# A two-block image network on one core: v's copies, weight preparation and the pacing of layer norms re-ordered

## The chip, the core and the metric

The kernel runs on one core of a Trainium2 chip. The time is that of the device, in microseconds, from the first to the last instruction of one launch; three runs of the kernel before give a median of 3362.36 us (3358.76 to 3363.83).

A core has five engines that run side by side, each with its own list of instructions in a fixed order: TensorE (PE) multiplies matrices, VectorE (DVE) and ScalarE (ACT) work element by element, GpSimd (POOL) and SyncE (SP) here mostly issue DMAs. They meet through semaphores: an instruction stands at the head of its engine's list until what it needs is there, and all that is behind it waits too.

## What is computed

Eight images of 384 channels and 32 x 32 places (1024 tokens) go through two blocks, all in float32:

```python
# block 0: attention and MLP on tokens
xn = layernorm(x, g1, beta1)
q, k, v = xn @ w_qkv.T + b_qkv                 # 8 heads of 48
x1 = softmax(q @ k.T * SCALE) @ v @ w_proj.T + b_proj + x
y = x1 + gelu(layernorm(x1, g2, beta2) @ w_fc1.T + b_fc1) @ w_fc2.T + b_fc2
# block 1: depthwise 7x7 convolution, norm, GELU, global response norm
z = layernorm(dwconv7x7(y) + dw_b, ln_w, ln_b)
z = gelu(z @ w1 + b1)
nx = l2norm_over_places(z); nx = nx / (mean(nx) + eps)
out = y + (gamma * z * nx + beta + z) @ w2 + b2
```

## The kernel before

**Layout.** Channels lie on the 128 partitions (three tiles of 128), tokens along the free dimension. An image's half is 512 tokens, a quarter of the first image 256. Attention works through two query halves (`qh`) times four pairs of heads (`m`) times eight key tiles (`t`). The exponential of scores runs on ScalarE, the convolution as 147 multiply-add taps for each image on VectorE.

**The order of work.** Images overlap: while TensorE does attention and the MLP of image b, VectorE convolves image b-1. The order of each engine's list is fixed when the program is built, by hand. Side work (a layer norm, a convolution, the preparation of weights) is written as a generator that yields how many us of matmul time to leave before its next step. `Flow.pe(us)` is called after each matmul, adds the normal time of it to a clock and lets all steps that are due write their instructions at this point of the program. So a longer wait moves a step further back in the lists, in whole matmul steps (0.857 us for one of 512 columns, 1.714 in `linear`); it doesn't make any engine idle by itself. `flow.finish` writes all remaining steps at once. `after(first, chain, us)` starts a chain when another one has ended. A chain spawned as `paced` counts its waits from the time when its last step was due.

**Layer norm.** `layernorm` has the same eight steps everywhere: two additions over the channel tiles (L406, L409), a sum over partitions by a matmul with ones (L374, or L388 when `fold` first halves the rows with a DMA, L382), subtraction of the mean (L416), squares on ScalarE (L423), their additions (L427, L430), the variance by a matmul, logarithm and exponential on ScalarE (L440, L441), and the scaling (L444). `slow` stretches some of its waits; `abreast` runs both halves side by side and stretches all of them by `factor`.

**The start.** `first_values` normalises image 0 in quarters, two steps apart, and computes v for each quarter (L521, two tiles of 128 tokens), copied out by ScalarE (L529).

**Weights prepared in image 0.** `folds` folds the norms' beta into biases: VectorE weighs the weights (L238, L240), TensorE sums them in columns (L244, 128x1 matmuls). `prepare(weights, False)` loads blocks of weights into the buffer `acc`, builds 15 sums of blocks ("forms", L1182, L1185) for a multiplication of matrices with fewer products, stores them in DRAM, and builds sums of w1. `prepare(weights, True)`, called `aside`, folds the last norm's bias through w1 (`shift_through_w1`, L1244 to L1253) in the buffer `xn`. Biases through w2 come from `shift_through_w2` (L1264 to L1271). `aside` must be finished before the second half's projection in attention, where `xn` is needed. `weights.release()` issues the ring's loads of the forms of fc2, which until then are held back. Before, `fc1_beta2`, the folds' sums, lies in `acc` too, so `preparing` waits for the folds to end.

**Averages.** `average` in attention adds the two halves of a product (L551, L553), sends the sums of the exponentials to DRAM and back (L557, L562, L573, L575, all issued by SyncE) and divides by them (L560, L579).

**The end.** Image 7's MLP runs in halves (`mlp_by_halves`): its second ln2 is spawned in the sixth matmul group of the first half, ln3 of image 6 follows it (`after(ln, norm)`), then the last convolution starts tile by tile in two parts of rows, followed by `norm_a` (part one), `norm_b` and `norm_c`.

Of the kernel before, what the change touches and what calls it, by code (L numbers as in the profile page):

```python
# [46 lines left out]
F32 = mybir.dt.float32  # L47
# [4 lines left out]
P = 128  # L52
B, C, H, W = 8, 384, 32, 32
N = H * W
CT = C // P
# [95 lines left out]
def block_kernel(  # L151
# [429 lines left out]
    def attention(b, xt, qT, kT, last_tile, first):  # L581
# [44 lines left out]
        for n in range(len(steps) + 2):  # L626
            if n == 2:
                last_tile()
            if n < len(steps):
                ps[n] = scores(*steps[n])  # L630
            if n >= 2:
                product(*steps[n - 2], ps.pop(n - 2))
            if n - 2 == len(steps) // 2 + 6:
                for chain in first:
                    flow.finish(chain)
                xn = one.tile([P, CT, N], F32, tag="xn", name=f"xn2_{b}")
                for m in (NP - 1, *range(CT)):
                    flow.finish(chains[0, m])
                proj(b, xt, 0)
                ln = flow.spawn(layernorm(xt, xn, 0, eps0, "g2", f"ln2_{b}", False, spaced=True, fold="columns"))  # L640

# [74 lines left out]
    def mlp(b, xt, xn, weights, tag, ln, rest, before_fc2):  # L716
# [5 lines left out]
        for m in range(HT):  # L722
            gelu_half(hid, m, 0, xn, weights, wa, f"fc1_{b}")
            if m == 3 and rest:
                rest()
                ln = flow.spawn(layernorm(xt, xn, 1, eps0, "g2", f"ln2_{b}", True))
        flow.finish(ln)
# [118 lines left out]
    def mlp_by_halves(b, xt, xn, weights, ln, rest, between):  # L846

        hid = one.tile([P, HT * N], F32, tag="big", name=f"hid_{b}").rearrange("p (m n) -> p m n", m=HT)
        for h in range(2):
            wa, wb = f"fc1_{b}_{h}", f"fc2_{b}_{h}"  # L850
            flow.finish(ln)
            for m in range(HT):
                gelu_half(hid, m, h, xn, weights, wa, f"fc1_{b}")
                if m % CM == CM - 1:
                    weights.used(wa, m // CM)
                if m == 5 and h == 0:
                    rest()
                    ln = flow.spawn(layernorm(xt, xn, 1, eps0, "g2", f"ln2_{b}", True))
                if m == 6 and h == 0:
                    between(0, -1, ln)  # L860
# [253 lines left out]
    def folds(weights):  # L1114

        t = two.tile([P, NH], F32, tag="r", name="wv_beta1")[:, :C]
        for k in range(CT):
            weighted(t, wv_sb[:, k, :], "beta1", k)
        u = one.tile([P, CT, N], F32, tag="acc", name="fc1_beta2").rearrange("p c n -> p (c n)")
        for m in range(HT):  # L1120
# [31 lines left out]
    def prepare(weights, aside):  # L1152

        def blocks(name, tag="acc"):
            t = one.tile([P, CT, N], F32, tag=tag, name=name).rearrange("p c n -> p (c n)")
            return t.rearrange("p (j k o) -> p j k o", j=4, o=P)
# [28 lines left out]
        def forms(name, w, store):  # L1187
# [30 lines left out]
            nc.gpsimd.dma_start(out=x, in_=block_of(w, 2, 3))  # L1218
            yield 18.0
            add(x, x, a33)  # L1220
# [14 lines left out]
        def shift_through_w1():  # L1235
            for i in range(0, HT // 2, CT):
# [3 lines left out]
                t = t.rearrange("p (i a o) -> p i a o", a=6, o=P)  # L1240
                yield 18.0
                for r, order in enumerate(((0, 1, 2), (5, 3, 4))):
# [11 lines left out]

        def shift_through_w2(which, tag):
            for r in which:
                t = blocks(f"w2_gbeta_{r}", tag)
                for s in range(2):
                    nc.gpsimd.dma_start(out=t[:, s], in_=chunk(w2, 2 * r + s).rearrange("p (k o) -> p k o", o=P))
                yield 12.0  # L1260
                h = HT // 2
# [11 lines left out]
        if aside:  # L1273
            yield from shift_through_w1()
            yield from shift_through_w2((0,), "xn")
            return
# [4 lines left out]
        for j, a in enumerate((0, 5, 3, 1)):  # L1281
            nc.gpsimd.dma_start(out=t[:, j], in_=tiles[:, :, a, :])
        yield 18.0
        sums(t)
        yield 4.0
        for j, key in enumerate(order):
            nc.gpsimd.dma_start(out=s_w1[:, :, int(key[1]) - 1, :], in_=t[:, j])
        yield from shift_through_w2((1, 2), "acc")
        yield from forms("w2", w2, s_w2)

    def first_values(xn):

        n = N // 4
        chains = [layernorm(xn, xn, slice(i * n, (i + 1) * n), eps0, "g1", "ln1_0", False) for i in range(4)]
        for step in range(2 * 3 + 8):
            for i, chain in enumerate(chains):
                if 0 <= step - 2 * i < 8:
                    next(chain, None)
            if step >= 7 and step % 2:
                i = (step - 7) // 2  # L1300
                values(0, xn, range(2 * i, 2 * i + 2))

    def main():
# [48 lines left out]
        def next_norms(b, ln=None):  # L1352
# [7 lines left out]
            if b + 1 < B:  # L1360
                xn = state["xn"] = load_x(b + 1, "xn")
                name = f"ln1_{b + 1}"
                places = (lambda: weight_places(name)) if b else averages
                norm = abreast(xn, xn, eps0, "g1", name, True, places=places, gentle=b > 0)
                state["norm1"] = flow.spawn(after(state["norm3"], norm, 50 if b else 14))

# [15 lines left out]
        def last_convolution(h, ct, ln=None):  # L1382
# [4 lines left out]
            if ct == 0:  # L1387
# [3 lines left out]
                if h == 0:  # L1391
                    state["norm_a"] = flow.spawn(after(state["conv"], last_norm(LAST[0], 2.0)))

        for b in range(B):
            if b == 0:
                folding = flow.spawn(after(None, folds(weights), 8))
                preparing = flow.spawn(after(folding, prepare(weights, False)))
                aside = flow.spawn(after(folding, prepare(weights, True), 4))
# [189 lines left out]
```

## Time and profile before

| | us |
|---|---|
| median of three runs | 3362.36 |
| profiled run, span | 3362.4 |
| TensorE busy | 3312.9 (99%) |
| VectorE busy | 2549.0 (76%) |
| ScalarE busy | 1423.8 (42%) |
| first q/k matmul of image 0 | 42.74 |
| first hidden layer (L345 x96 in the chain) of image 1 | 552.40 |
| the same of image 2 | 956.60 |
| last group of matmuls of the chain, from | 3289.37 |

A line of a timeline gives the start, the duration, the engine, the line, the operation, what is written and read, the shape, how many, and in brackets the idle time before and who ended it. Matmuls are pipelined and their ends are modelled: a busy TensorE can still run below its full rate. Each 512-column float32 matmul shows as two records.

### The profile page before, as it was taken

How to read it: one execution, taken by the hardware profiler on the slowest of the kernel's cores; microseconds unless marked ns; L12 is line 12 of the kernel's file. 1: busy time of each engine (PE TensorE's matmuls, PEld its weight loads, DVE VectorE, ACT ScalarE, POOL GpSimd, SP SyncE). 2: the span in 40 equal slices, each digit the busy share in tenths (PEclk: the TensorE clock that was granted, in tenths of full speed). 3: DMA queues.
4: the chain of work that ended last, by engine and by line, in shares of the span. 5: the costliest groups of instructions: out<-in, count | busy, mean ns of one | idle time of the engine just before them, and what ended most of it. 6: DMA issues, size and time to landing. Idle time of an engine off the chain costs nothing.

```text
span 3362.4 us, 37483 instructions
## 1 busy us (share of the span) xinstructions
PE 3312.9 (99%) x14282; PEld 1422.0 (42%) x14282; DVE 2549.0 (76%) x3133; ACT 1423.8 (42%) x1886; POOL 208.3 (6%) x243
## 2 busy tenths in 40 slices
PE   8999999999999999999999999999999999999999
PEld 4334434443344433444334443444434444344455
DVE  3353789778878878778787796977888779989940
ACT  2442353353534345343543525426254353531641
POOL 1121000100001000000001000010000110000000
PEclk9899999999999999999999999999999999999999
DMA  3435201632125411355105350062501633123231
GB/s 123 142 125 143 65 20 34 172 86 84 24 61 153 110 53 23 83 136 126 33 18 123 102 137 18 15 145 90 132 17 35 172 81 97 20 55 89 61 96 51
DMA packets 151243, 281.59 MB, mean 84 GB/s; under 512 B 35216, under 2 KB 41232, under 8 KB 150672
## 3 DMA queue, kind: packets, MB, share of 16 engines
q1 hardware_dynamic: 114704, 201.32, 19.9%
q0 software_dynamic: 36064, 77.08, 11.9%
q8 instruction: 115, 1.88, 0.2%
q10 hardware_dynamic: 288, 0.71, 0.1%
q14 instruction: 72, 0.59, 0.1%
HBM read 181.52 MB, written 33.82 MB: 64 GB/s over the span
## 4 chain that ended last, share of the span: by engine, by line
PE 87%; DVE 9%; DMA 2%; ACT 1%; issue 1%; SPq 0%; POOL 0%; DVEq 0%; ACTq 0%; POOLq 0%
PE fc L345 12%; PE s L592 12%; PE o L612 11%; PE fc_p L352 10%; PE h L352 10%; PE o_p L352 9%; PE qk L332 6%; PE v L521 4%; PE o L997 4%; DVE acc L894 3%; PE proj L535 3%; DVE wqkv L894 3%; PE h_last L1041 1%; PE h L332 1%; PE qk_last L345 1%
## 5 line engine op out<-in xcount | busy, mean ns | idle before, releaser
L894 DVE SCALAR_TENSOR_TENSOR acc<-pad,vec,acc 128x1024 f32<-128x1024 f32 x1008 | 1230.2, 1274 | 0.0
L601 ACT ACTIVATE p<-s 128x1024 f32<-128x1024 f32 x512 | 523.6, 1024 | 390.3 <-PE s L592 387.9
L592 PE MATMUL s<-qk 48*64 48x512 f32 x4096 | 547.2, 595 | 2.0 <-ACT qk L495 1.5
L612 PE MATMUL o<-p,v 64*64 64x512 f32 x4096 | 541.8, 592 | 0.0
L345 PE MATMUL fc<-xn,fc 128*128 128x512 f32 x1152 | 503.1, 595 | 1.4 <-DVE x L714 1.4
L345 PEld LDWEIGHTS fc<-xn,fc 128*128 128x128 f32 x1152 | 218.9, 191 | 282.0 <-issue 268.6
L352 PE MATMUL fc_p<-hid,fc 128*128 128x512 f32 x728 | 318.2, 592 | 0.0
L612 PEld LDWEIGHTS o<-p,v 64*64 64x64 f32 x4096 | 160.5, 133 | 286.1 <-issue 279.9
L592 PEld LDWEIGHTS s<-qk 48*64 48x64 f32 x4096 | 156.9, 133 | 286.9 <-issue 262.6
L364 ACT ACTIVATE hid<-fc,bfc_f 128x512 f32<-128x512 f32 x192 | 130.7, 686 | 343.4 <-PE fc L345 343.3
L942 DVE TENSOR_TENSOR y<-h,y 128x512 f32<-128x512 f32 x288 | 197.0, 689 | 97.8 <-PE h L352 87.3
L352 PE MATMUL o_p<-y,w 128*128 128x512 f32 x624 | 270.9, 592 | 0.0
L352 PEld LDWEIGHTS fc_p<-hid,fc 128*128 128x128 f32 x728 | 138.2, 190 | 174.8 <-issue 169.5
L332 PE MATMUL qk<-xn,wqkv 128*128 128x512 f32 x480 | 207.4, 592 | 0.0
L352 PE MATMUL h<-acc,w_A 128*128 128x512 f32 x432 | 206.4, 596 | 0.0
L894 DVE SCALAR_TENSOR_TENSOR wqkv<-pad,vec,wqkv 128x416 f32<-128x416 f32 (+1 forms) x288 | 193.6, 744 | 0.6
L352 PEld LDWEIGHTS o_p<-y,w 128*128 128x128 f32 x624 | 118.0, 190 | 148.7 <-issue 133.5
L553 DVE TENSOR_TENSOR attn<-o,attn 128x512 f32<-128x512 f32 x64 | 44.0, 688 | 153.7 <-ACT attn L551 153.6
L495 ACT ACTIVATE qk<-qk,bqk 128x1024 f32<-128x1024 f32 x40 | 44.6, 1114 | 229.0 <-PE qk L332 229.0
L332 PEld LDWEIGHTS qk<-xn,wqkv 128*128 128x128 f32 x480 | 91.1, 190 | 114.1 <-issue 112.1
L710 ACT COPY pad<-x 128x512 f32<-128x512 f32 x48 | 30.2, 634 | 252.7 <-DVE x L774 190.1
L521 PE MATMUL v<-wqkv,xn 128*128 128x384 f32 x384 | 130.3, 497 | 5.0 <-DVE xn L444 5.0
(296 smaller groups left out, 3345.6 us busy)
## 6 DMA issues: line engine op xcount, KB each, us to landing
w_A<-in_w SPq DMA_DIRECT2D x72, 384.0 KB, 3.2
fc<-s_fc SPq DMA_DIRECT2D x91, 256.0 KB, 2.9
hid<-hid POOLq DMA_DIRECT2D x42, 512.0 KB, 6.9
fc<-in_wfc SPq DMA_DIRECT2D x54, 384.0 KB, 5.8
w<-s_w SPq DMA_DIRECT2D x78, 256.0 KB, 2.7
y<-y POOLq DMA_DIRECT2D x36, 512.0 KB, 6.9
kept<-x SPq DMA_DIRECT2D x8, 1536.0 KB, 8.1
xn<-in_x SPq DMA_DIRECT2D x14, 768.0 KB, 6.8
```

Source lines behind the costliest of these rows:

```text
L332: nc.tensor.matmul(out=ps[:, half(h)], lhsT=lhsT(k), rhs=rhs(k)[:, half(h)], start=(k == 0), stop=(k == nk - 1),)
L345: nc.tensor.matmul(out=ps, lhsT=lhsT(k), rhs=rhs(k)[:, half(h)], start=(k == 0), stop=(k == nk - 1))
L352: nc.tensor.matmul(out=bank, lhsT=lhsT, rhs=rhs, start=k == 0, stop=k == len(pairs) - 1)
L364: nc.scalar.activation(dst, src, function, **kw)
L521: nc.tensor.matmul(out=ps[:, :C], lhsT=xn[:, k, t * P : (t + 1) * P], rhs=wv_sb[:, k, :], start=(k == 0), stop=(k == CT - 1),)
L535: nc.tensor.matmul(out=ps, lhsT=wproj_sb[:, m, ct * P : (ct + 1) * P], rhs=attn[:, m, :], start=(m == 0), stop=(m == CT - 1),)
L592: nc.tensor.matmul(out=s[64 * i : 64 * i + 64, j, :], lhsT=kT[64 * j : 64 * j + HD, m, k0 : k0 + 64], rhs=qT[64 * j : 64 * j + HD, m, half ...
L601: nc.scalar.activation(p, s, AF.Exp)
L612: nc.tensor.matmul(out=outs[i][64 * j : 64 * j + 64, :], lhsT=v[keys, t, at : at + 64], rhs=p[keys, j, :], start=(t == 0), stop=(t == KT - 1),
L894: nc.vector.scalar_tensor_tensor(dst, window, tap, dst, ALU.mult, ALU.add)
L942: nc.vector.tensor_tensor(dst, bank, part, ALU.add)
L997: nc.tensor.matmul(out=ps, lhsT=tiles[k], rhs=y(k, part), start=(k == 0), stop=(k == HT - 1))
```

## The change

It has three parts.

1. `first_values`: v of a quarter is written one step later, after the logarithm and exponential of the next quarter's norm.
2. Preparation: `fc1_beta2` goes into `attn` (not yet used then) in place of `acc`, so that `preparing` starts on its own after 4 us of matmul time, beside the folds; the whole of `shift_through_w2` is done in `preparing`, and `aside` keeps the w1 part alone; most waits before the use of a load grow by 2 to 7 us.
3. Longer waits between the steps of some layer norms: ln2 of images 1 and 7, ln1 of image 1 (which also starts after 11 instead of 14 us), and `norm_a`.

```diff
-                ln = flow.spawn(layernorm(xt, xn, 0, eps0, "g2", f"ln2_{b}", False, spaced=True, fold="columns"))
+                slow = 1.4 if b in (1, B - 1) else 1.0
+                ln = layernorm(xt, xn, 0, eps0, "g2", f"ln2_{b}", False, spaced=True, slow=slow, fold="columns")
+                ln = flow.spawn(ln)
...
-                ln = flow.spawn(layernorm(xt, xn, 1, eps0, "g2", f"ln2_{b}", True))
+                slow = 1.2 if b == 1 else 1.0
+                ln = flow.spawn(layernorm(xt, xn, 1, eps0, "g2", f"ln2_{b}", True, slow=slow))
...
-                    ln = flow.spawn(layernorm(xt, xn, 1, eps0, "g2", f"ln2_{b}", True))
+                    ln = flow.spawn(layernorm(xt, xn, 1, eps0, "g2", f"ln2_{b}", True, slow=2.0))
...
-        u = one.tile([P, CT, N], F32, tag="acc", name="fc1_beta2").rearrange("p c n -> p (c n)")
+        u = attn.rearrange("p m n -> p (m n)")
...
             nc.gpsimd.dma_start(out=x, in_=block_of(w, 2, 3))
-            yield 18.0
+            yield 25.0
...
                 nc.gpsimd.dma_start(out=t, in_=w1[:, i * 6 * P : (i + CT) * 6 * P])
                 t = t.rearrange("p (i a o) -> p i a o", a=6, o=P)
-                yield 18.0
+                yield 22.0
...
-        def shift_through_w2(which, tag):
-            for r in which:
-                t = blocks(f"w2_gbeta_{r}", tag)
+        def shift_through_w2():
+            for r in range(CT):
+                t = blocks(f"w2_gbeta_{r}")
...
-                yield 12.0
+                yield 14.0
...
             yield from shift_through_w1()
-            yield from shift_through_w2((0,), "xn")
             return
...
-        yield 18.0
+        yield 22.0
         sums(t)
...
-        yield from shift_through_w2((1, 2), "acc")
+        yield from shift_through_w2()
...
-        for step in range(2 * 3 + 8):
+        for step in range(2 * 3 + 9):
...
-            if step >= 7 and step % 2:
-                i = (step - 7) // 2
+            if step >= 8 and step % 2 == 0:
+                i = (step - 8) // 2
...
-                norm = abreast(xn, xn, eps0, "g1", name, True, places=places, gentle=b > 0)
-                state["norm1"] = flow.spawn(after(state["norm3"], norm, 50 if b else 14))
+                norm = abreast(xn, xn, eps0, "g1", name, True, places=places, gentle=b > 0, factor=1.4 if b else 1.7)
+                state["norm1"] = flow.spawn(after(state["norm3"], norm, 50 if b else 11))
...
-                    state["norm_a"] = flow.spawn(after(state["conv"], last_norm(LAST[0], 2.0)))
+                    state["norm_a"] = flow.spawn(after(state["conv"], last_norm(LAST[0], 2.6)))
...
-                preparing = flow.spawn(after(folding, prepare(weights, False)))
+                preparing = flow.spawn(after(None, prepare(weights, False), 4))
```

## The prediction

> **What bounds the kernel now.** I read the page first, then the chain of waits, TensorE's own waits, and timelines of the stretches those point to.
>
> ```profile
> PE 3312.9 (99%) x14282; PEld 1422.0 (42%) x14282; DVE 2549.0 (76%) x3133; ACT 1423.8 (42%) x1886; POOL 208.3 (6%) x243
> ```
>
> TensorE hardly ever stops, so time can only come out of its gaps. The chain of waits shows where these are not:
>
> ```profile
> 552.40 41.20 PE fc L345 x96
> 956.60 41.20 PE fc L345 x96
> 1360.80 41.20 PE fc L345 x96
> ```
>
> The first hidden layer starts every 404.2 us, and does so up to 2573.41: images 2 to 6 repeat. The losses lie in the start, image 0, the first norms of image 1, and image 7. TensorE's waits name them:
>
> ```profile
> PE ln_sum L374 <- DVE ln_a L409: 13.6, 5, 5.7
> PE v L521 <- DVE xn L444: 5.0, 3, 2.0
> PE b L244 <- DVE b_f L1253: 4.3, 2, 3.6
> PE b L244 <- DVE w_gbeta L1267: 3.5, 1, 3.5
> PE ln_var L388 <- DMA ln_sq<-ln_sq: 2.8, 3, 1.6
> PE h L332 <- ACT h L973: 2.3, 1, 2.3
> ```
>
> (Columns: total us, times, longest.) They understate the cost. A full 128x512 matmul record ends 0.43 us after the one before it; taking each record's step from the previous end less this normal step (a quarter of it for the 64x64 tiles) I get 98 us of loss in all, 18.8 of them between 105 and 190 us, where the waits show 8.3. The rest is slow running after a wait:
>
> ```profile
> 143.33 1.44 PE L244 MATMUL b<-ones,w_lnb 128*128 128x1 f32 x6 [3.63 <-DVE b_f L1253]
> 144.70 1.98 PE L592 MATMUL s<-qk 48*64 48x512 f32 x8
> 149.28 1.03 PE L612 MATMUL o<-p,v 64*64 64x512 f32 x8
> ```
>
> The same eight records take 1.98 us after the wait and 1.03 a few us later.
>
> **What the Trainium skill says.** "TensorE: Matmul & The Clock Gate", Part 1, What's actually happening: after an idle window of about 3.4 us TensorE's clock is halved, and it takes about as long of work to come back. The trace agrees on the halving (1.98 against 1.03); here even the 2.3 us of tiny matmuls at 109.08 to 111.42 bring it on, while the 1.58 us wait at 335.69 does not. Same page, Architectural detail: VectorE and ScalarE are strict first-in-first-out queues; the trace agrees, ScalarE stands still 7.21 us behind one square (below). "DMA: Bandwidth & Descriptors", Anatomy of one DMA: a semaphore is waited for by the issuing sequencer, not by the DMA engine; SyncE's 9.33 us (below) is that.
>
> **The start (`first_values`).** Before, v's matmuls of a quarter and their two copies come, in program order, ahead of the next quarter's logarithm and exponential:
>
> ```profile
> 21.73 0.48 ACT L529 COPY v<-v 128x384 f32<-128x384 f32 x1 [1.46 <-PE v L521]
> 22.11 0.48 ACT L440 ACTIVATE ln_rstd<-ln_var,eps 128x256 f32<-128x256 f32 x1
> 23.61 4.14 PE L521 MATMUL v<-wqkv,xn 128*128 128x384 f32 x12 [1.54 <-DVE xn L444]
> 35.82 5.83 PE L521 MATMUL v<-wqkv,xn 128*128 128x384 f32 x12 [1.97 <-DVE xn L444]
> ```
>
> The variance was ready at 14.15 but L440 runs at 22.11, behind the copies. TensorE then waits for L440, L441 and L444. One step later the exponential goes first, so the next quarter's xn is normalised while this quarter's v runs. Walking the new order by these durations: v of quarter 0 ends at 21.5 as before, variance 2 at 22.1, v1 to 26.2, variance 3 to 26.8, v2 to 31.0, v3 to 35.1, against 41.65. The inputs hold: quarter 2's L444 ends near 25.6, quarter 3's near 29.5, and wqk_beta (2.7 us on VectorE) near 32.2, before TensorE wants it at 35.1. **Saved 6.4**, on q/k's first matmul: the 5.0 of three waits and the cold clock of the last quarter (5.83 to 4.14, 1.7), less some 0.3 of hand-over. The early loads of the preparation join 8.67 MB that land by 23 us at some 390 GB/s; 1.5 MB more is 4 us, and nothing here reads what lands last before 29.
>
> **Folds and preparation (image 0).** The sums of fc1_beta2 move into attn, so `preparing` no longer waits for the folds: its first forms run on VectorE beside the folds, where it was idle from 57 to 73 us. Before, forms, w1 shift and averages met in one queue. The worst meeting:
>
> ```profile
> 137.52 9.33 SPq L276 DMA_DIRECT2D fc<-s_fc  x3
> 159.61 0.69 DVE L579 TENSOR_TENSOR attn<-attn,r 128x512 f32<-128x512 f32 x1 [14.64 <-DMA r<-back]
> 167.54 0.35 PE L244 MATMUL b<-ones,w_gbeta 128*128 128x1 f32 x2 [3.47 <-DVE w_gbeta L1267]
> ```
>
> The ring's loads at `weights.release()` wait in SyncE for the last form's store; behind them queue the averages' back and r; L579 on VectorE waits for r; behind L579 queue w_gbeta's products; TensorE's column sum waits for those. In the change the release comes some 35 us earlier, between two averages, with its forms (about 5.6 us of VectorE) done soon after the first average's reciprocal, and this w2 part moves to after the first proj. So I take off the 3.47, its slow running (1.8) and the late proj behind it (1.8 with the former). The two w1 column sums stay: 12 tiny matmuls each (about 1.5 us) with a VectorE copy between. The waits of 22 rather than 18 put them about a quarter of attention away from the first forms, but the second meets an average whose r takes 6 to 7 us from its reciprocal while 5.1 is planned. Both together cost 12 to 13 of the 18.8 today; I leave them 5 (bounds 2 and 11), and the three small w2 sums 1 to 2. 18.8 - 6.5 = **12 saved**, bounds 5 and 16. The tiny sums bfc and bout at 76.87 to 82.54 and the cold clock after them (5.5) stay.
> Longer waits cost nothing by themselves: nothing waits for `preparing` but its finish behind the MLP of image 0. Adding its waits, rounded up to the matmul steps, gives 196 us after the q/k projection starts; image 0's MLP ends about 270 after. Its later forms fall into the first hidden layer, where VectorE idles.
>
> **Image 1's norms.** `factor` 1.7 with a start 3 us earlier: in steps of 0.857 us the variance sum comes two steps (1.7) later, the first sum one earlier; the DMA fold lands by then: 1.58 + 0.24 saved, **1.7**; L444 still ends 5 us before v. In attention (`slow` 1.4) two waits grow by a step, so 1.7 more for an overdue of 1.2, but convolution taps (1.2 us each) slip in ahead on VectorE: **0.7** of 1.8. fc1 (1.2): one step, **0.4** of 1.2. Image 7's attention, likewise, **0.8** of 1.6.
>
> **Image 7, second ln2 (`slow=2.0`).**
>
> ```profile
> 2979.06 2.07 PE L374 MATMUL ln_sum<-ln_a,ones 128*128 128x512 f32 x2 [3.75 <-DVE ln_a L409]
> 2980.93 9.13 PE L345 MATMUL fc<-xn,fc 128*128 128x512 f32 x16
> ```
>
> Three more steps before the sum leave 1.1 of the 3.75 and keep the clock (9.13 to 6.9): 5.7 at this place. But VectorE has no slack here: from 3009.57 to 3230 it idles under 5 us. The last waits also push ln3 of image 6 (chained behind ln2) past the start of the last convolution, so ln3's sums queue behind some 16 taps (11 us) there: I find its variance wanted at 3014 and ready at 3019. And TensorE waits at 3039.54 for x L714 (1.42) anyway. VectorE's own work is the same. Net **0** (bounds -3 and +3).
>
> **`norm_a`, 2.0 to 2.6.**
>
> ```profile
> 3113.82 1.55 ACT L423 ACTIVATE ln_sq<-wqkv 128x416 f32<-128x416 f32 x3 [7.21 <-DVE wqkv L416]
> 3117.60 7.11 PE L332 MATMUL h<-acc,w_A 128*128 128x512 f32 x12 [2.33 <-ACT h L973]
> ```
>
> The squares wait for L416, the GELU of the third tile queues behind them on ScalarE, and TensorE's fifth tile wants that bank. Steps here are 1.714: 0.8 x 2.0 = 1.6 is one, 0.8 x 2.6 = 2.08 is two, so the squares pass behind that GELU and the bank is free at 3112. The loss is 4.3 (2.3, and slow running 2.0). Near the end norm_b's sum is ready 4.3 us before TensorE (3230.4 to 3234.73), so the gain isn't given back there. ln3's shifts can move norm_a one step; I take **3.3** (bounds 0 and 4.3).
>
> **Sum.** 6.4 + 12 + 1.7 + 0.7 + 0.4 + 0.8 + 0 + 3.3 = 25.3; 3362.4 - 25.3 = 3337.1, say 3337.
>
> **Rivals.** (a) Preparation's waits only move: averages, w1 shift and sums still meet in VectorE's queue. For it: r takes longer than planned and forms meet the first w1 shift again. Against: the SyncE block is what made the 14.64. Then 5 for that part, and image 7 gives 1: 3362.4 - 6.4 - 5 - 2.8 - 1 = 3347. (b) Only the start gains: image 7's ln3 turns into a cold wait (-3) and the preparation pays for itself in new waits: 3357 to 3360, within 0.2%. (c) Slower: forms ahead of the folds delay bfc, or a load into acc holds GpSimd's queue and with it ln2's fold DMAs, 15 us or more: 3370. Against: the folds end 20 us before TensorE wants them, and forms add 7. (d) Everything falls away, 5 more in image 0 and 3 in image 7: 3329.
>
> **Chances.** Forecast 0.55, (a) 0.22, (b) 0.08, (c) 0.05, (d) 0.10. Range 3328 to 3351: (d) and (a) with 4 us for unforeseen waits, leaving out (b) and (c). Faster by over 6.7 us: forecast, (a), (d) and a part of (b), 0.89; within 0.05; slower 0.06.
>
> **What would show it.** q/k's first matmul near 36.3 instead of 42.74. No TensorE wait on w_gbeta L1267, no L579 wait near 14 us, column sums of w_lnb waiting under 3. The 3.75 at ln_sum gone to about 1, but a new TensorE wait at ln3's variance. No wait on h L973. The forecast falls if column sums wait over 5 us in all, or if fc1 of image 1 (552.40) comes less than 15 us earlier.

## The result, and the profile after

The changed kernel takes 3348.59 us (median of 4 runs, 3346.73 to 3348.89) where the kernel before takes 3362.97 (4 runs, 3358.76 to 3363.83). The ratio is 0.9959, with a 95% interval of 0.9941 to 0.9976: faster by 14.4 us, where 25.3 were forecast.

The other engines' busy times hardly move (first part of the page, changed kernel). TensorE's falls by 9.3 us, from 3312.9, with the same 14282 records, and its gaps by 6.5, from 49.5 to 43.0. So more than half of the profiled gain of 15.8 is records that run faster, as the prediction's slow running behind a wait lets expect, and the rest is gaps:

```profile
PE 3303.6 (99%) x14282; PEld 1416.7 (42%) x14282; DVE 2550.6 (76%) x3133; ACT 1421.0 (42%) x1884; POOL 208.1 (6%) x243
```

TensorE's waits in the changed kernel (total us, times, longest):

```profile
PE ln_sum L374 <- DVE ln_a L409: 12.9, 5, 6.3
PE ln_var L374 <- DVE ln_sq L430: 8.7, 8, 5.9
PE b L244 <- DVE b_f L1256: 3.6, 2, 3.3
PE ln_var L388 <- DMA ln_sq<-ln_sq: 2.2, 3, 1.2
PE proj L535 <- DVE attn L579: 2.1, 1, 2.1
```

Three rows of before are gone: `xn L444` (5.0), `w_gbeta` (3.5) and `h L973` (2.3). One is new, a projection that waits 2.1 for attention's average L579, and one has grown: the variance sums, which waited 3.9 in all and 1.8 at most, now wait 8.7, and one of them 5.9. The column sums still wait 3.3 in the place where they waited 3.6 before.

Where the time came from is best seen by following one point after another through the program. The order of each product's records is the same in all kernels, so the n-th record of a product is the same work everywhere, and its end can be compared. The table gives how much earlier than before it ends in us (a minus sign is earlier), worked out from the traces by counting TensorE's records; a change from one column to the next is what that stretch won or lost. The points are: v of image 0; the end of attention in image 0; v of image 1; the second projection of image 1; the end of fc1 of image 1; the middle of image 7's attention; the end of the first half of image 7's MLP (`half 7`); the 864th record of h, behind `norm_a`; the end. Each kernel's one trace is set against the one trace of before, so the table shows single executions.

```
                              v 0    att 0    v 1   proj 1   fc1 1  att 7  half 7  h 864    end
changed kernel              -6.60  -17.91  -17.36  -13.18  -14.14 -14.01  -10.37 -14.43  -15.83
e4_start_alone              -6.55   -8.37   -5.55   -5.55   -5.60  -5.60   -6.95  -8.64   -6.09
e5_preparation_alone        +0.73   -7.98   -8.45   -8.43   -8.78  -8.77   -8.64  -8.62   -8.63
e1_image1_attention_wait..  -6.50  -17.55  -15.25  -15.03  -14.51 -14.44   -9.48 -13.54  -14.94
e2_image1_ln1_back          -7.25  -15.94  -16.00  -14.77  -14.25 -14.21   -9.18 -14.59  -16.00
e8_image1_all_back          -6.74  -18.08  -18.73  -18.72  -18.87 -18.87  -13.51 -17.65  -19.05
e3_image7_ln2_back          -6.73  -17.80  -17.74  -16.82  -16.30 -16.30  -15.33 -15.36  -15.36
e9_image7_first_wait_only   -6.36  -17.47  -15.20  -14.34  -13.83 -13.84  -15.16 -16.17  -14.63
e10_norm_a_back             -6.74  -17.99  -17.76  -16.39  -15.88 -15.81  -10.33 -15.86  -15.93
e11_half_rows_in_conv_a     -7.47  -15.96  -15.85  -14.87  -14.35 -14.22  -15.51 -21.57  -23.62
e7_w1_sums_later            -7.03  -16.63  -13.14  -13.07  -12.89 -12.89   -8.22 -13.35  -14.75
e12_chosen_waits            -7.59  -16.32  -16.88  -16.87  -16.77 -16.75  -17.54 -18.55  -21.63
e13_later_stores            -7.78  -17.21  -13.79  -13.50  -13.32 -13.19  -14.48 -13.78  -16.86
```

The first row holds the result: 6.6 at the start, 11.3 more by the end of attention in image 0, then 3.8 lost in image 1 where 2.8 were to be won, nothing from image 2 to the middle of image 7 (0.1), and 1.8 won in the rest of image 7 where 4.1 were forecast.

The start, TensorE's timeline of the changed kernel:

```profile
22.42 0.59 PE L374 MATMUL ln_var<-ln_sq,ones 128*128 128x256 f32 x2
22.85 4.03 PE L521 MATMUL v<-wqkv,xn 128*128 128x384 f32 x12
26.72 0.59 PE L374 MATMUL ln_var<-ln_sq,ones 128*128 128x256 f32 x2
27.15 7.90 PE L521 MATMUL v<-wqkv,xn 128*128 128x384 f32 x24
34.89 1.40 PE L244 MATMUL bqk<-ones,wqk_beta 128*128 128x1 f32 x12
36.15 26.00 PE L332 MATMUL qk<-xn,wqkv 128*128 128x512 f32 x60
```

No bracket: from variance 2 on nothing waits, and q/k's first product starts at 36.15 (42.74 before). The last two quarters of v run at one speed, 7.90 us for 24 records, where the last alone took 5.83 before.

Image 0's column sums, TensorE's timeline of the changed kernel:

```profile
105.36 0.83 PE L244 MATMUL b<-ones,w_lnb 128*128 128x1 f32 x6 [0.25 <-DVE b_f L1256]
106.12 1.09 PE L592 MATMUL s<-qk 48*64 48x512 f32 x8
137.95 1.44 PE L244 MATMUL b<-ones,w_lnb 128*128 128x1 f32 x6 [3.32 <-DVE b_f L1256]
139.32 1.98 PE L592 MATMUL s<-qk 48*64 48x512 f32 x8
151.65 0.38 PE L244 MATMUL b<-ones,w_gbeta 128*128 128x1 f32 x2
```

The first w1 sum is now free of a wait and keeps the clock (eight records in 1.09), the second is not and doesn't (1.98), and the one on w_gbeta waits for nothing.

What the second one waits for stands in VectorE's timeline of the same kernel:

```profile
115.16 0.20 DVE L560 RECIPROCAL inv<-sums 128x8 f32<-128x8 f32 x1 [8.17 <-DMA sums<-attn]
121.66 0.69 DVE L579 TENSOR_TENSOR attn<-attn,r 128x512 f32<-128x512 f32 x1 [6.30 <-DMA r<-back]
137.14 0.69 DVE L579 TENSOR_TENSOR attn<-attn,r 128x512 f32<-128x512 f32 x1 [6.68 <-DMA r<-back]
137.75 0.15 DVE L1256 TENSOR_TENSOR b_f<-b,vec 128x3 f32<-128x3 f32 x1
```

The copy L1256 has its sums at 134.6, where TensorE ends them, but L579 stands ahead of it in VectorE's list and waits for r until 137.14. TensorE's next six tiny products want the copy. The 14.64 of before is gone: SyncE still stands on the release (9.65 us, from 94.73), but earlier, and now L579 waits 6 to 7 us.

### The profile page after: what moved, and what is told of

It reads as the page before. It is cut to its first block, busy times and chain, and to the rows that moved or that the text cites. A ratio compares the mean times of both kernels' runs of the same rounds, so it can differ in the third digit from the quotient of the medians.

```text
span 3346.6 us, 37477 instructions
## 1 busy us (share of the span) xinstructions
PE 3303.6 (99%) x14282; PEld 1416.7 (42%) x14282; DVE 2550.6 (76%) x3133; ACT 1421.0 (42%) x1884; POOL 208.1 (6%) x243
## 4 chain that ended last, share of the span: by engine, by line
PE 87%; DVE 10%; DMA 2%; issue 1%; ACT 0%; SPq 0%; POOL 0%; DVEq 0%; POOLq 0%
PE o L612 12%; PE s L592 12%; PE fc L345 12%; PE h L352 10%; PE fc_p L352 10%; PE o_p L352 9%; PE qk L332 6%; DVE wqkv L897 4%; PE v L521 4%; PE o L1000 4%; PE proj L535 3%; DVE acc L897 3%; PE h_last L1044 1%; PE qk_last L345 1%; PE ln_var L374 1%
## 5 line engine op out<-in xcount | busy, mean ns | idle before, releaser
L535 PE MATMUL proj<-attn,wproj_sb 128*128 128x512 f32 x288 | 129.2, 602 | 2.1 <-DVE attn L579 2.1
```

Source lines behind the costliest of these rows:

```text
L535: nc.tensor.matmul(out=ps, lhsT=wproj_sb[:, m, ct * P : (ct + 1) * P], rhs=attn[:, m, :], start=(m == 0), stop=(m == CT - 1),)
```

## The experiments

Each kernel is the changed one with the edit shown, unless it says otherwise. A single run of it stands beside runs of the kernel before on the same chip; where there are four or five runs, a ratio is given. The expectations forecast the span of the profile, which is 1.7 to 1.9 us shorter than the time of the same run. The changed kernel, e7, e8, e12 and e13 stay within some 2 us of their medians, before within 6 (3356.78 to 3366.31 in nine runs on one chip), so where there is a single run its time alone decides little, and the trace carries the verdict.

### Start and preparation apart

`e4_start_alone` is the kernel before with the new `first_values` alone; `e5_preparation_alone` keeps the preparation and takes back the start and all waits of the norms.

```diff
# e4, against the kernel before
-        for step in range(2 * 3 + 8):
+        for step in range(2 * 3 + 9):
-            if step >= 7 and step % 2:
-                i = (step - 7) // 2
+            if step >= 8 and step % 2 == 0:
+                i = (step - 8) // 2
# e5, against the changed kernel: the same edit undone, and
-                slow = 1.4 if b in (1, B - 1) else 1.0
+                slow = 1.0
-                slow = 1.2 if b == 1 else 1.0
+                slow = 1.0
-layernorm(xt, xn, 1, eps0, "g2", f"ln2_{b}", True, slow=2.0)
+layernorm(xt, xn, 1, eps0, "g2", f"ln2_{b}", True)
-factor=1.4 if b else 1.7)
+factor=1.4)
-50 if b else 11
+50 if b else 14
-last_norm(LAST[0], 2.6)
+last_norm(LAST[0], 2.0)
```

> Before with first_values' edit alone. Theory A (the gain of the start is TensorE's own and nothing later gives it back): q/k of image 0 ends 6.0 to 7.3 us earlier than before, and the same 6 to 7 are there at the end: 3355 to 3356. Theory B (what follows in image 0 hangs on VectorE, which the start doesn't free): the gain shrinks to under 3 by the first hidden layer of image 0.

> Before with the preparation's edits alone (sums in attn, preparing after 4 us, all of w2 in it, longer waits); start and norms as before. Theory A (the parts add up): image 0's first hidden layer begins 11.3 us earlier than before, and the norms of image 1 and image 7 cost what they cost before, so that 3351 comes out. Theory B (the earlier preparation itself brings waits into image 1): the wait of proj on attn L579, or ln_sum L388 on its fold, appears here, and 3353 to 3356 comes out.

e4: 3358.08 us in one run, beside 3362.96 for before (7 runs). The start wins 6.55 at v and has 6.1 at the end. e5: 3355.54 in one run, beside 3361.07. By the end of attention in image 0 it has won 8.7 from where v left it (+0.73 to -7.98), and keeps it to the end. Together 14.7 by the traces, close to the changed kernel's 15.83 at the end. By the times beside before it is less, 4.9 and 5.5, together 10.4 of 14.4. So the two parts bring most of the gain, and the waits of the norms together between one and four microseconds, which single runs can't settle. Both kernels keep to the end what they had after image 1, as e4's theory A has it. e5's profiled span, 3353.8, lies in the range of its theory B, but neither wait that B names is in its trace: image 0 alone gave less, 8.0 by the end of its attention where 11.3 was expected.

### Image 1's norms

Three kernels take back the waits there: attention's ln2 alone, ln1 alone, and all three.

```diff
# e1
-                slow = 1.4 if b in (1, B - 1) else 1.0
+                slow = 1.4 if b == B - 1 else 1.0
# e2
-factor=1.4 if b else 1.7)
+factor=1.4)
-50 if b else 11
+50 if b else 14
# e8: both of these, and
-                slow = 1.2 if b == 1 else 1.0
+                slow = 1.0
```

> The changed kernel with slow = 1.0 again in image 1's attention norm, all else kept. In the changed kernel image 1's second proj loses 4.0 us against before (TensorE waits 2.08 for attn L579, and loses clock), which the prediction had not. Theory A (the longer wait moves L444 behind the first L579 in VectorE's list, so that VectorE stands 1.83 and 3.38 us on r and the last average comes late): without it the wait on L579 is gone and the proj of image 1 ends 3.5 to 4.5 us earlier; the variance wait in attention stays at about 1.2 to 1.5, total 3342 to 3343. Theory B (the shift of image 0 by the preparation changed the phase of convolution taps or DMA): the 2.08 stays, total within 1 us of 3346.6.

> The changed kernel with ln1 of image 1 as before (factor 1.4, start after 14). The changed kernel loses 0.55 us between the first hidden layer of image 0 and v of image 1 where 1.7 was to be won: the sum's DMA fold is now waited for (0.92) and the product it falls into runs cold. Theory A (the start 3 us earlier puts the sum ahead of its fold; factor 1.7 itself does good): here the 0.92 goes and the 1.58 on the variance comes back, net -0.5 to +0.5 us of 3346.6. Theory B (the wait follows image 0's new preparation): a wait of 0.5 or more at ln_sum L388 stays.

> The changed kernel with all three edits of image 1's norms undone (ln1 with factor 1.4 after 14, attention 1.0, first hidden layer 1.0); start, preparation and image 7 as changed. Theory A (these edits cost what image 1 lost): from the first hidden layer of image 0 (17.9 earlier than before) to that of image 2 nothing is lost, so that 17 to 18 are there in image 2 where the changed kernel has 14.1, and the time is about 3345. Theory B (image 1's losses come from DMAs that land early or late, run by run): 14 to 16.5, no better than 3347.

e1: 3349.22 in one run, e2: 3348.26 in one run (before 3361.07). e8: 3346.04 (4 runs, 3345.13 to 3346.52), ratio to before 0.9948 (0.9932 to 0.9965). With all three waits back the kernel enters image 1 18.1 us ahead of before and leaves it 18.9 ahead: nothing is lost, where the changed kernel loses 3.8. Its time is 2.6 below the changed kernel's median, with no run of either in the other's range (it was measured beside other runs of before, which took 3362.96).

What one kernel loses over the whole of image 1 doesn't show what the norms' waits cost: e7 and e13 (below), which also have all three back, lose 3.7 and 3.9 there. The stretches do. e7 and e13 lose it ahead of v of image 1. From there to the end of fc1, where the edits of attention's and fc1's ln2 act, the six kernels with both edits (changed, e2, e3, e9, e10, e11) lose 1.4 to 3.2 us, and the six with neither (e4, e5, e7, e8, e12, e13) lose at most 0.5. So these two edits are a loss in every kernel that has them. e1, without attention's, loses 0.7 there; its span, 3347.4, misses the 3342 to 3343 of its theory A all the same, since it loses 2.3 ahead of v and wins 1.3 less than the changed kernel in image 7.

The largest single loss is at the second projection. TensorE's timeline of the changed kernel:

```profile
517.48 7.97 PE L535 MATMUL proj<-attn,wproj_sb 128*128 128x512 f32 x14 [2.08 <-DVE attn L579]
537.99 1.12 PE L374 MATMUL ln_var<-ln_sq,ones 128*128 128x512 f32 x2 [0.52 <-DVE ln_sq L430]
```

and of the kernel with the three waits back:

```profile
512.02 7.89 PE L535 MATMUL proj<-attn,wproj_sb 128*128 128x512 f32 x18
532.40 1.12 PE L374 MATMUL ln_var<-ln_sq,ones 128*128 128x512 f32 x2 [1.18 <-DVE ln_sq L430]
```

Fourteen records behind a wait of 2.08 against eighteen in one go. The cause shows in VectorE's list, at attention's last three averages ahead of this projection. The changed kernel:

```profile
488.96 0.69 DVE L579 TENSOR_TENSOR attn<-attn,r 128x512 f32<-128x512 f32 x1 [1.83 <-DMA r<-back]
489.57 2.07 DVE L444 SCALAR_TENSOR_TENSOR xn<-xn,vec,ln_rstd 128x512 f32<-128x512 f32 x3
...
505.25 0.69 DVE L579 TENSOR_TENSOR attn<-attn,r 128x512 f32<-128x512 f32 x1 [3.38 <-DMA r<-back]
...
516.74 0.69 DVE L579 TENSOR_TENSOR attn<-attn,r 128x512 f32<-128x512 f32 x1 [0.56 <-DMA r<-back]
```

and in the kernel before:

```profile
502.08 2.07 DVE L444 SCALAR_TENSOR_TENSOR xn<-xn,vec,ln_rstd 128x512 f32<-128x512 f32 x3
...
506.46 0.68 DVE L579 TENSOR_TENSOR attn<-attn,r 128x512 f32<-128x512 f32 x1
...
519.87 0.69 DVE L579 TENSOR_TENSOR attn<-attn,r 128x512 f32<-128x512 f32 x1 [2.49 <-DMA r<-back]
...
531.43 0.69 DVE L579 TENSOR_TENSOR attn<-attn,r 128x512 f32<-128x512 f32 x1 [0.64 <-DMA r<-back]
```

Before, ln2's normalising L444 stood ahead of the first L579 and filled 2.07 us of r's trip; this L579 then waited for nothing. With 1.4, L444 stands behind it, and VectorE idles 1.83 there. Together with the two that follow it idles 5.77 us in place of 3.14, and so comes late to the last average, which TensorE waits for. In all six kernels with 1.4, L444 stands behind the first L579, VectorE idles 4.16 to 5.77 at the three, and the projection waits (2.08, 0.97, 0.82, 0.57, 0.49, 0.47). In all eight with 1.0 (before among them) L444 stands ahead of it, VectorE idles 2.8 to 3.6, and the projection doesn't wait. In each of the six the wait is the idle time less 3.7 us: so much lead VectorE has, and what it idles beyond that TensorE pays. The wait thus belongs to this edit.

What the edit was to cure stayed: attention's variance sum waits 1.20 to 1.22 in the kernels with 1.4 and 0.94 to 0.97 in those with 1.0. The fc1 edit does no better: its variance waits 1.14 to 1.18 with 1.0 (before, e4, e5, e7, e8, e12, e13) and 1.51 or 1.52 with 1.2 (e1, e2, e3, e9, e10, e11). The changed kernel's own 0.52 (above) is the exception; perhaps the 2.08 that TensorE had just stood at the projection gave VectorE time.

For ln1 the runs show no effect. From the end of attention in image 0 to v of image 1, kernels with the new waits change by +0.55, +2.30, +0.06, +2.27, +0.23 and +0.11 (changed, e1, e3, e9, e10, e11); with the old ones by +2.82, -0.47, -0.06, +3.49, -0.65 and -0.56 (e4, e5, e2, e7, e8, e12; e13, whose last projection in image 0 was late as well, by +3.42). Two groups, about 0 and about +2.3 to 3.5, and both occur with either setting. With the old waits the variance sum waits 1.76 in e8 and 1.84 in e7, which come out of this stretch 4.1 apart; behind it e7's next four records, after 0.35 more of waiting, take 1.97 us, e8's 1.07: slow running, not the wait, makes most of the difference. With the new waits the sum splits: 0.92 at the first sum, then 0.37 and 0.67 at the two variances in the changed kernel, 1.96 together, where the forecast left nothing. In e2, as its theory A expects, the 0.92 is gone, the variance waits 1.97, and the span, 3346.4, is the changed kernel's within 0.2.

### Image 7: the second ln2, and `norm_a`

e3 takes `slow=2.0` back; e9 lengthens only the first wait of that norm (and leaves the others at 1.0); e10 takes `norm_a` back to 2.0.

```diff
# e3
-layernorm(xt, xn, 1, eps0, "g2", f"ln2_{b}", True, slow=2.0)
+layernorm(xt, xn, 1, eps0, "g2", f"ln2_{b}", True)
# e9
-        yield 2.6 * slow
+        yield 2.6 * slow * first
-layernorm(xt, xn, 1, eps0, "g2", f"ln2_{b}", True, slow=2.0)
+layernorm(xt, xn, 1, eps0, "g2", f"ln2_{b}", True, first=2.0)
# e10
-last_norm(LAST[0], 2.6)
+last_norm(LAST[0], 2.0)
```

> The changed kernel with slow 1.0 again in the second ln2 of image 7, norm_a and all else kept. Theory A, that of the prediction (VectorE bounds image 7 from its ln2 on, so that the 5.7 won at ln_sum only returns at ln3's variance, 5.92): ln_sum waits about 3.7 again, the 5.92 is gone, and the end is within 1.5 us of 3346.6. Theory B (the longer waits cost more than they win, by the cold clock behind ln3's variance): the end comes 2 to 4 us earlier. Theory C (they win): 2 us or more later.

> The changed kernel, in whose second ln2 of image 7 only the wait before the first sum is doubled, and the later ones are 1.0. Theory A (VectorE sets image 7's time at fixed points, and TensorE's gains between them only turn into waits): ln_sum waits about 2.5, ln3's variance less than 2 in place of 5.92, the first half of the MLP ends 3 to 5 us earlier than in the changed kernel, but the third quarter of h (its 864th record) comes within 1 us of the changed kernel's, and norm_b's variance waits about 2 again, so that the end is the same or up to 2 us later. Theory B (the gain carries): the end comes 3 us or more earlier.

> The changed kernel with norm_a at 2.0 again. Theory A (norm_a's edit is worth what the wait on h L973 cost, where ln2's longer waits are kept): TensorE waits 1 to 2.5 for h L973 again in place of 1.40 for norm_a's variance, and h's 864th record comes 1 to 4 us later, counted from the entry of image 7. Theory B (its wait only changes its name): h's 864th record comes within 0.7 us of the changed kernel's, counted from there.

Each ran once: e3 3348.81 (before 3361.07), e9 3349.60 (before 3362.96), e10 3348.24 (before 3362.52). The sum and the two variances concerned, TensorE's timeline of the changed kernel:

```profile
2966.45 1.12 PE L374 MATMUL ln_sum<-ln_a,ones 128*128 128x512 f32 x2 [2.43 <-DVE ln_a L409]
3006.97 2.07 PE L374 MATMUL ln_var<-ln_sq,ones 128*128 128x512 f32 x2 [5.92 <-DVE ln_sq L430]
3110.01 0.96 PE L374 MATMUL ln_var<-ln_sq,ones 128*128 128x416 f32 x2 [1.40 <-DVE ln_sq L430]
```

The sum waits 2.43, the variance of ln3 5.92 and runs cold after it. Why it is late, VectorE, same kernel:

```profile
2990.40 6.15 DVE L897 SCALAR_TENSOR_TENSOR wqkv<-pad,vec,wqkv 128x416 f32<-128x416 f32 x9
2996.47 3.67 DVE L416 SCALAR_TENSOR_TENSOR acc<-ln_sum,acc 128x512 f32<-128x512 f32 x6
3000.05 5.46 DVE L897 SCALAR_TENSOR_TENSOR wqkv<-pad,vec,wqkv 128x416 f32<-128x416 f32 x8
3006.22 0.69 DVE L430 TENSOR_TENSOR ln_sq<-ln_sq,ln_sq 128x512 f32<-128x512 f32 x1
```

Seventeen taps of the last convolution stand ahead of ln3's two steps, 11.6 us. In e3, whose ln2 is not held back, the sum waits 4.80 and the 5.92 is gone: from the middle of image 7's attention to the end of the first half of the MLP it loses 1.0 (16.30 to 15.33) where the changed kernel loses 3.6. But it wins nothing afterwards.

A lead at the entry of image 7 is carried to the end, so ends are to be counted from there. Five kernels have the changed kernel's image 7 (changed, e1, e2, e7, e8); from the middle of its attention to the end they win 0.2 to 1.9, and e3 loses 0.9. By this count the longer waits are worth 1.1 to 2.8 us, 1.4 of it behind the 864th record of h, where each of the five wins 1.40 and e3 nothing.

e9 has a short wait at both places: sum 1.90, ln3's variance 1.18; the first half of the MLP ends 4.8 us earlier than the changed kernel's (15.16 and 10.37). Behind that TensorE waits 2.15 for x L716 and runs slowly after it, and loses more near the end, so that from its entry on it wins 0.8, no more than the five. (At the 864th record of h it is 1.7 ahead of the changed kernel, where its theory A expected less than 1.) There norm_b's variance waits in e9:

```profile
3224.41 0.75 PE L374 MATMUL ln_var<-ln_sq,ones 128*128 128x288 f32 x2 [1.77 <-DVE ln_sq L430]
```

and VectorE of e9 shows what it waits behind:

```profile
3222.68 0.75 DVE L1008 SCALAR_TENSOR_TENSOR res<-o,b_f,res 128x512 f32<-128x512 f32 x1 [2.25 <-PE o L1000]
3223.90 0.46 DVE L430 TENSOR_TENSOR ln_sq<-ln_sq,ln_sq 128x288 f32<-128x288 f32 x1
```

In the changed kernel the two stand the other way about:

```profile
3221.81 0.46 DVE L430 TENSOR_TENSOR ln_sq<-ln_sq,ln_sq 128x288 f32<-128x288 f32 x1
3225.06 0.75 DVE L1008 SCALAR_TENSOR_TENSOR res<-o,b_f,res 128x512 f32<-128x512 f32 x1 [2.80 <-PE o L1000]
```

The last output tile's eviction L1008 waits for its product; if L430 stands behind it, so does norm_b. That order is a by-product of `slow=2.0`: a norm that ends later changes when the convolution's emission ends, and with it where norm_b's steps fall. norm_b's variance waits 1.77 in every kernel without `slow=2.0` and with the old norm_b (before, e3, e4, e5, e9) and in no other. From the 864th record of h to the end the order is worth 1.4 us beside e3 and 2.9 beside e9, and nobody aimed at it.

e10 gives `norm_a`'s worth. Its program is the changed kernel's up to norm_a, so it is to be counted from the last point ahead of that, the end of the first half of the MLP. From there e10 wins 5.5 by the 864th record of h and 5.6 by the end; the five kernels with norm_a at 2.6 win 4.1 to 5.4 and 5.5 to 6.8. So the edit is worth nothing at the 864th record and between nothing and 1.2 us at the end. TensorE's wait on h L973, 2.3 before, is gone in the changed kernel, but the 1.40 at norm_a's own variance (above) has taken its place; e10 has neither wait, and instead 1.7 at a later one (gmean L1061).

### Is VectorE the bound of image 7?

e11 is the changed kernel with the first part of the last convolution cut to about half; it leaves out six of the thirteen rows there, so it doesn't compute the whole network:

```diff
# e11, in convolution
+        if y1 < H:
+            y1 = 7
```

> The changed kernel, in which the first part of the last convolution writes 7 of its 13 rows (the rest of these rows is left out), so that VectorE's taps there take about 0.35 in place of 0.57 to 0.69 us, at the same places of the program. Theory A (VectorE's backlog is what TensorE meets at ln3's variance and at norm_a): the wait of 5.92 at ln3's variance falls to under 2, the one of 1.40 at norm_a's variance goes, and the span is 6 to 10 us shorter than 3346.6. Theory B (the order of the lists or ScalarE is the cause): the 5.92 falls by less than 2.

3340.55 in one run (before 3362.52). TensorE, e11:

```profile
3002.93 1.12 PE L374 MATMUL ln_var<-ln_sq,ones 128*128 128x512 f32 x2 [2.32 <-DVE ln_sq L430]
```

ln3's variance waits 2.32 for 5.92 (not quite the "under 2" of theory A), norm_a's for nothing, and from the middle of image 7's attention to the end this kernel wins 9.4 where the changed one wins 1.8. Fewer taps on VectorE alone did this: these two waits of TensorE in image 7 are VectorE's backlog.

### The second w1 sum

e7 is e8 with the column sums put 2.5 us of matmul time later, so that the copy comes behind the average; e13 is e12 (below) with a longer wait ahead of the stores of w1's sums, to see whether they slow r.

```diff
# e7, against e8
-                yield 5.0
+                yield 7.5
# e13, against e12: after sums(t)
-        yield 4.0
+        yield 12.0
```

> As the run before, and in shift_through_w1 the wait before the column sums is 7.5 in place of 5.0. The second w1 sum of the changed kernel waits 3.32 for b_f, which stands behind L579 (6.68 on r) in VectorE's list, and 2 more are lost in cold clock. Theory A (order alone): the sums come two to three steps later each, behind that L579, the wait falls under 1 us, and 4 to 5 us are won in image 0: about 3341. Theory B (the next meeting, with the products of w_gbeta, takes its place): a wait of 2 or more on b_f stays, and the time is that of the run before within 1.5 us.

> The run before, with 12 in place of 4 us between the sums of w1 and their four stores of 384 KB. Theory A (the stores stand in the DMA engines ahead of the third average's r, which holds L579, and L579 holds b_f): r lands earlier, the second w1 sum waits under 1 us in place of about 3, and 4 to 5 us are won in image 0: 3336 to 3339. Theory B (r is late for its own length, back and forth through DRAM): the wait stays over 2 and the time is that of the run before within 1.5 us.

e7: 3348.48 (4 runs), ratio 0.9954 (0.9937 to 0.9970): 2.4 slower than e8 in the median, with no run of either in the other's range. The sum still waits 3.11, for another reason. VectorE, e7:

```profile
137.26 0.69 DVE L579 TENSOR_TENSOR attn<-attn,r 128x512 f32<-128x512 f32 x1 [10.39 <-DMA r<-back]
137.87 0.48 DVE L1247 TENSOR_SCALAR w_lnb<-w_lnb,vec 128x384 f32<-128x384 f32 x1
...
144.06 0.11 DVE L1256 TENSOR_TENSOR b_f<-b,vec 128x3 f32<-128x3 f32 x1
```

Now w1's products (L1247, L1249) queue behind the same late average, and the copy behind the next reciprocal: a move of 2.5 us went from one side of a wait to the other and met the next. e13: 3345.50 (5 runs), ratio 0.9949 (0.9935 to 0.9962), 3.6 slower than e12. L579 waits 6.11 and the sum 3.56 (6.77 and 2.07 in e12). But the edit didn't do what it was meant for. GpSimd issues the four stores at 127.37 in e13 and at 127.12 in e12: nothing stands ahead of them in its list, so a later place there doesn't hold them back, and they go as soon as VectorE has made the sums. What the longer wait moved is the work behind it, w2's part. In e13 an average of the second half then waits 9.26 for its r (5.34 in e12), and the last projection of image 0 waits 1.31 for its last average; why is not shown. So whether the stores make r late is not tested. SyncE in e13, at the loads of r:

```profile
131.30 1.66 SPq L575 DMA_DIRECT2D r<-back  x1
133.01 1.62 SPq L573 DMA_DIRECT2D r<-back  x1
```

Each of the two stands 1.6 us in SyncE (1.33 and 1.17 in e12). What holds them, and what makes r late, stays open.

### A choice of waits

e12 is e8 (image 1 as before) with e9's edit (only the first wait of image 7's ln2 longer) and norm_b's waits cut, so that its squares stand ahead of L1008.

```diff
# e12, against e8: e9's edit, and
-last_norm(LAST[1], 1.0)
+last_norm(LAST[1], 0.7)
```

> Start and preparation as changed; image 1's norms as before; image 7's attention 1.4 and norm_a 2.6 as changed; its second ln2 with the first wait alone doubled; norm_b's slow 0.7, so that its additions come ahead of the last output tile's eviction in VectorE's list. Theory: image 2 begins 18 to 19 us earlier than before, ln3's variance waits under 2, norm_b's variance not at all, and 2 to 4 us more are won in image 7: 3340 to 3343. If norm_b's order doesn't matter, its variance waits 1.8 again and 3344 to 3346 comes out.

3341.94 (5 runs, 3340.84 to 3343.86; before 3362.52 in nine runs); ratio to before 0.9940 (0.9926 to 0.9954). It is the fastest kernel that computes the whole network, 6.7 below the changed kernel's median, with no run of either in the other's range. TensorE, e12:

```profile
2994.96 1.13 PE L374 MATMUL ln_var<-ln_sq,ones 128*128 128x512 f32 x2 [1.18 <-DVE ln_sq L430]
3220.09 0.65 PE L374 MATMUL ln_var<-ln_sq,ones 128*128 128x288 f32 x2
```

ln3's variance waits 1.18 (5.92 in the changed kernel) and norm_b's for nothing, because its square (3217.90) now passes L1008 (3220.30). Image 7 wins 4.9 from the middle of its attention (3.7 in e13, which has the same image 7), where e9 won 0.8 and the changed kernel 1.8. In image 2 the lead is 16.8, not the 18 to 19 of the forecast: image 0 brought less in this run.

## Why the prediction was right in sign and 11 us too good

**The start: right.** 6.4 forecast, 6.6 measured, and 6.1 left at the end with this part alone. q/k's first product comes at 36.15, forecast 36.3. The walk of the new order by old durations held, the cold last quarter included. One reading in it was off without bearing on it: 8.67 MB is what had moved by 75 us; by 23 us it was some 8.0 (347 GB/s).

**Folds and preparation: right in size, by its own account.** 12 forecast, 11.3 measured; the kernels with both parts show 8.5 to 11.3, and e5 8.7 when the start is left as it was. The wait on w_gbeta, its slow running and the late projection are gone; L579's 14.64 has become 6.7. "I leave them 5" for the two w1 sums was close: the first costs nothing, the second 6.4 us of loss between 135 and 145. The reason given for it, an r that takes 6 to 7 us from its reciprocal where 5.1 is planned, is what the trace shows, but r took longer still there (126.71 to 137.14, 10.4 us), and moving the sums didn't cure it. What makes r late is not shown. Rival (a) falls as a whole, since this part brought 8.5 to 11 and not 5, though at the second w1 sum its picture is the right one: average, w1 shift and sum still meet in VectorE's queue. (The line of 1.03 us that the prediction sets beside s's 1.98 is that of the other product, o; s takes 1.03 there too.)

**Image 1's norms: the step that failed.** The prediction added 1.7, 0.7 and 0.4; the changed kernel's trace shows a loss of 3.8. Most of the surplus lies here. By the records' ends the changed kernel is 15.8 ahead, 9.5 short of the forecast, and 6.6 of these are image 1's. The sums counted how many steps a wait grows and what it was overdue by; they did not ask what else stood in VectorE's list at the places where the norm's instructions would come to lie. For attention (0.7) the text named "convolution taps slip in ahead" and stopped there. What changed places was L444, which had filled r's trip: behind the first average it left VectorE idle, and TensorE paid 0.47 to 2.08 at the projection, with slow running 0.9 to 4.2 from v to there, in all six kernels with this edit and in none without. For fc1 (0.4) the variance waited longer, 1.5 for 1.18, in every kernel but one, and with it 0.5 was lost from the projection to the end of fc1. So where 1.1 was to be won by these two edits, 1.4 to 3.2 was lost. For ln1 (1.7) the wait was split over three sums, and the runs show no effect that stands out of a scatter of some 4 us. e8, with all three back, is 2.6 faster; this alone would not do as proof, since e7's move in image 0 takes 2.4 away again.

**Image 7, second ln2: right in mechanism and nearly in size.** "Net 0", because ln3's variance would be "wanted at 3014 and ready at 3019": it was late by 5.92, for the reason given, seventeen taps for "some 16". The sum's wait fell to 2.43, not to 1.1. What the prediction did not see is norm_b, whose better place wins 1.4. Counted from the entry of image 7 the edit is worth 1.1 to 2.8 beside e3, inside the stated bounds. The part of it that is norm_b's was luck.

**`norm_a`: mis-sized.** The 2.33 on h L973 is gone as forecast, and no more. norm_a's variance waits 1.40 instead, a wait that was not there before and that goes when VectorE has fewer taps (e11): VectorE's backlog again, which the prediction named one paragraph earlier and did not apply here. Beside e10, nothing of the 3.3 shows at the 864th record of h, and at most 1.2 at the end. Image 7's attention (0.8) brought 0.1.

**The sum** by the records' ends is 6.6 + 11.3 - 3.8 - 0.1 + 1.8 = 15.8, where 25.3 stood; the medians give 14.4, since the profiled execution of before (3364.16) lies 1.2 above its median. Of the two stated signs that the forecast falls, one came in part: fc1 of image 1 starts 15.8 us earlier, since two of its records now stand ahead of the variance that waits, but ends only 14.1 earlier. The other did not come: column sums wait 3.6 in all, though one of w_lnb waits 3.3 where under 3 was forecast. The outcome is closest to rival (a)'s number, 3347, and mainly for another reason than rival (a)'s.

## What to carry to other kernels

A longer wait between two steps of a chain moves the chain's instructions to another place in an in-order queue; before it is priced by the wait it removes, look at what stands in that queue on both sides of the new place, who hides whose trip there, and whether the engine has any slack at all. Where it has none, as VectorE in image 7, a wait shortened in one norm comes back in the next, and only less work (e11) or a better order at the one place that matters (e12, which lengthens the first wait alone and shortens norm_b's) gains much. Check in the trace, too, that an edit moved what it was to move: a later place in a list holds nothing back where nothing stands ahead of it (e13). And test a bundle of small edits piece by piece: here two parts brought most of the gain, the longer waits of the norms together 1 to 4 us, and those in image 1, taken alone, were a loss.

## What the runs showed of the hardware

- Whether a short idle costs TensorE its clock is not a matter of that idle's length alone. "TensorE: Matmul & The Clock Gate" of the Trainium skill, Part 1, What's actually happening, speaks of an idle window of about 3.4 us, and says that the window runs freely and isn't reset by a kernel's start; where it stood is not shown here. Here a lull of tiny products with short waits halves the rate after 2.3 us (before, 109.08 to 111.42) and not after 1.85 (changed kernel, 104.28 to 106.12); and waits of 1.76 and 1.84 us at the same place in ln1 of image 1 are followed by records at full rate in e8 and, after 0.35 more, at half rate in e7. An edit worth less than the 4 us between those two can't be judged from one such place in one run.
- A small transfer can take long. The transfer of attention's sums took 2 us at 92.11 to 94.07 and let VectorE go only 8 us after its issue at 107.01 (the 8.17 at 115.16), while loads of whole weight tiles were under way. That these hold it up is a guess; no run took them away.
